# Row sums of the second layer: from four 64x32 tiles of the PE array to all eight, each head's product split by halves of the block's nodes

## The chip, the cores and the metric

The kernel runs on one core of one Trainium2 chip. Its time is device microseconds of one execution. The engines of a core work side by side: TensorE (PE in the profile; PEld is its weight loads), VectorE (DVE), ScalarE (ACT), GpSimd (POOL) and SyncE (SP), each with its own queue of instructions. They wait for one another through semaphores. Matrix products go from on-chip memory (SBUF) into eight banks of accumulators (PSUM, 512 f32 columns by 128 partitions each); DVE and ACT read those, POOL does not.

## The reference

Four graph layers are stacked over 4096 nodes of 256 features, with one 4096 x 4096 0/1 adjacency; after each layer comes `x = layernorm(x + layer(x, adj))`. All is f32. The change lies in the second layer, a multi-head attention with four heads of 64 features:

```
q, k, v = heads(x @ Wq + bq), heads(x @ Wk + bk), heads(x @ Wv + bv)
scores = einsum('hnd,hmd->hnm', q, k) / sqrt(64) + (edge.T - 1) * 10000
attn = softmax(scores, axis=-1)
ctx = einsum('hnm,hmd->hnd', attn, v)
```

The kernel makes the softmax without a maximum per row: it takes the exponential of the scores less one common shift, multiplies by the 0/1 edge and divides at the end by the sum of a row. That sum, one number for each node and head, is what "row sums" means here.

## The kernel before

The four layers follow one another; `additive_heads`, `multi_head_attention`, `additive_one` and `cosine_attention` hold them. Each works block by block: a block is 512 nodes (`QW`, four groups `QB` of 128), and there are eight blocks. In the second layer the other side of the attention is taken 64 nodes at a time, in 64 steps `j` for each block.

A step of the second layer has three parts. `scores` (L578) makes four 64x64 products, one on each quarter of the PE array, into a PSUM tile `p` of two banks: partitions are two halves `c` of 64 neighbours, `r` is the bank, and head `2c + r` (`KC * c + r` in the code) lies at half `c` and bank `r`. ACT takes the exponential in place (L580). `weights` multiplies by the edges on DVE into `prob` (L590) and adds up `prob` for the row sums in `den[b]`: for even `j` with an addition on POOL (L597), for odd `j` with an accumulating DMA that POOL's queue issues (L603). `sums` (L611), three steps later, multiplies `prob` by the values into two accumulator banks. In the steady state PE alternates four matmuls of L578 with four of L611.

While the next block runs, `finish` ends the block before it at fixed steps. At steps 7 and 9 DVE joins the three parts of `den` (L620). At step 12 `row_sums` sums `den` over the 64 partitions of a half: a product with a 64x32 block of ones for each head puts the head's sum for all 512 nodes on 32 equal partitions, and ACT copies the 128 x 512 result to `kept[b][2]` (L630). At step 15 `turned_row_sums` transposes that in four 128x128 pieces (L635), `turned_half` transposes two groups of outputs (L642), `reciprocals` (L648) reads one of every 32 columns into `rden`, and `half` divides (L653) and adds to the features (L656). Step 18 does the other two groups. Later steps make the layernorm; there the small DVE instructions L136 to L139 (`end_root`) refine a square root, and L150 (`begin_root`) begins it.

`halves()` takes one `p` tile, two banks, out of the same pool of three that `scores` uses, and gives out its banks one by one; it is released when the last reader of either bank is done. So a score matmul three allocations later waits for it.

In the loop of the layer the order on PE, DVE and ACT is the order of the code (`manual_schedule`). POOL and SP, and everything in the next layer, are ordered by the scheduler. The last block's end, `tail`, runs inside the third layer: there `bank()` gives one of four banks, and the instructions stand between the third layer's matmuls (L418), its exponential part on ACT (L410) and its weights on DVE (L412).

Of the kernel before, what the change touches and what calls it, by code (L numbers as in the profile page):

```python
# [20 lines left out]
KC = D // P  # L21
QB = 4
QW = QB * P
# [5 lines left out]
def kernel(  # L29
# [27 lines left out]
    nc = tc.nc  # L57
# [14 lines left out]
    ones = const.tile([P, P], FP, name="ones")  # L72
# [398 lines left out]
    def multi_head_attention(w_sb, b_sb, tail, rows_of_den, narrow_edges):  # L471
# [6 lines left out]
        d = D // H  # L478
        G = P // H
# [3 lines left out]
        kept, den, rden, mvs, roots = {}, {}, {}, {}, {}  # L483
        with ExitStack() as lay:
# [7 lines left out]
            with ExitStack() as pro:  # L492
# [6 lines left out]
                def bank():  # L499
                    return ps.tile([P, QW], FP, name="g")  # L500
# [119 lines left out]
                eng.tensor_tensor(den[b][:, 0, :], den[b][:, 0, :], den[b][:, n, :], OP.add)  # L620

            def row_sums(bank, b):
                pd = bank()
                for r in range(KC):
                    for c in range(KC):
                        h = KC * c + r
                        half = slice(c * d, (c + 1) * d)
                        nc.tensor.matmul(pd[h * G:(h + 1) * G, :], ones[half, :G], den[b][half, 0, r * QW:(r + 1) * QW],
                                         start=True, stop=True)
                nc.scalar.copy(kept[b][KC], pd)  # L630

            def turned_row_sums(bank, b):
                pd = bank()
# [11 lines left out]

            def reciprocals(pd, b):
                rden[b] = fin.tile([P, QB, H], FP, name="rden4")
                nc.vector.reciprocal(rden[b].rearrange("p k h -> p (k h)"), pd[:, ::G])  # L648

            def half(po, b, k):  # L650

# [12 lines left out]
            def finish(b, j):  # L664

                rows = [X[:, b * QB + k, :D] for k in range(QB)]
                if j in (7, 9):
                    join_sums(b, j // 2 - 2)
                elif j == 12:
                    row_sums(halves(), b)  # L670
                elif j == 15:
                    bank = halves()
                    pd = turned_row_sums(bank, b)
                    po = turned_half(bank, b, 0)
                    reciprocals(pd, b)
                    half(po, b, 0)
                elif j == 18:
                    half(turned_half(halves(), b, 2), b, 2)
                elif j in (21, 23, 25, 27):
                    k = (j - 21) // 2  # L680
                    if k == 0:
                        mvs[b] = fin.tile([P, QB, 2], FP, name="mv")
                    one_row(mvs[b], k, rows[k])
                elif j == 29:
                    roots[b] = begin_root(mvs[b])
                elif j == 33:
                    end_root(*roots[b])
                elif j in (35, 37, 39, 41):
                    k = (j - 35) // 2
                    scale_row(rows[k], mvs[b], roots[b][1], k)  # L690
# [6 lines left out]
            with tc.manual_schedule(engines=fixed):  # L697
                for i in range(len(units) + LAG):
                    b, j = units[i - LAG] if i >= LAG else (-1, 0)
# [11 lines left out]
        def tail(bank):  # L711
            b = NB - 1
            join_sums(b, 1, nc.gpsimd)
            join_sums(b, 2, nc.gpsimd)
            row_sums(bank, b)
            reciprocals(turned_row_sums(bank, b), b)
            for k in (0, 2):
                half(turned_half(bank, b, k), b, k)
            mv = fin.tile([P, QB, 2], FP, name="mv")
            for k in range(QB):  # L720
                one_row(mv, k, X[:, b * QB + k, :D])
            layernorm_block(b, mv)
# [216 lines left out]
```

## Time and profile before

| what | value |
|---|---|
| median of five runs | 2940.95 us (2939.52 to 2943.2) |
| the profiled execution's own time | 2940.95 us |
| its span | 2939.1 us |
| granted PE clock | 1.00 |
| span of the second layer's loop | about 823 to 1730 us |
| PE busy in the span | 2916.8 us, 99% |
| row-sum matmuls (L628) | 64 records in eight calls |
| ACT copies of the row sums (L630) | 585 ns in the loop, 566 ns in the tail |
| reciprocals (L648) | 248 ns in the loop, 258 ns in the tail |

PE's records overlap where it works on several tiles at once, so the length of a record is not its cost; the distance between the starts of two groups is. The profile prints the shape of a tile as rows*columns (64*32), then the moving operand (64x512). A bracket behind a line gives the idle time of that engine just before it, and who ended it.

### The profile page before, as it was taken

The numbers are of one execution on the slowest core, as the hardware profiler recorded it, in microseconds if no ns is written. First come the engines' busy times: TensorE is split into PE (matmuls) and PEld (weight loads), VectorE is DVE, ScalarE is ACT, GpSimd is POOL, SyncE is SP. The second block draws the span as 40 slices with busy tenths as digits, with TensorE's granted clock in tenths as the row PEclk, the third lists the DMA queues.
The fourth block names the chain that finished last, engine by engine and source line by source line (L and its number), as shares of the span: only waits on it lengthen the run. The fifth ranks groups of instructions, "written<-read, shape, count | busy, mean of one in ns | idle before, by whom it ended". The sixth has DMA issues, their size and how long they took to land.

```text
span 2939.1 us, 50968 instructions
## 1 busy us (share of the span) xinstructions
PE 2916.8 (99%) x20591; PEld 1565.7 (53%) x20591; DVE 1942.0 (66%) x2488; ACT 1668.5 (57%) x2606; POOL 928.3 (32%) x647
## 2 busy tenths in 40 slices
PE   9999999999999999999999999999999999999998
PEld 5333333333643333333333358888887777777776
DVE  7899999997467777877877865555555333333333
ACT  7899999997356666666666654444444222222222
POOL 1000010100068888888889860000000000000000
PEclk9999999999999999999999999999999999999999
DMA  7566666764068888889889877555552343333331
GB/s 197 106 137 137 137 141 141 143 124 83 1 144 190 185 183 189 180 186 190 179 189 187 179 159 140 154 151 151 152 132 53 49 59 58 58 58 58 58 58 29
DMA packets 207166, 374.91 MB, mean 128 GB/s; under 512 B 15073, under 2 KB 90833, under 8 KB 206034
## 3 DMA queue, kind: packets, MB, share of 16 engines
q0 software_dynamic: 102304, 177.77, 38.4%
q1 hardware_dynamic: 104352, 193.62, 21.9%
q8 instruction: 161, 2.64, 0.4%
q14 instruction: 75, 0.61, 0.1%
q10 hardware_dynamic: 274, 0.26, 0.0%
HBM read 317.00 MB, written 21.04 MB: 115 GB/s over the span
## 4 chain that ended last, share of the span: by engine, by line
PE 97%; DVE 2%; ACT 1%; issue 0%; DVEq 0%; ACTq 0%
PE acc L266 23%; PE acc L810 15%; PE p L578 14%; PE acc L611 14%; PE acc L418 8%; PE g L418 7%; PE p L799 4%; PE g L799 3%; PE g L510 2%; PE g L176 1%; PE g L524 1%; PE acc L176 1%; PE g L118 1%; PE acc L761 1%; DVE s L138 1%; DVE prob L590 1%
## 5 line engine op out<-in xcount | busy, mean ns | idle before, releaser
L590 DVE TENSOR_TENSOR prob<-p,mask 128x1024 f32<-128x1024 f32 x512 | 623.1, 1223 | 202.4 <-ACT p L580 198.2
L580 ACT ACTIVATE p<-p,shift 128x1024 f32<-128x1024 f32 x512 | 556.3, 1088 | 333.8 <-PE p L578 333.0
L266 PE MATMUL acc<-prob,V 128*32 128x512 f32 x6144 | 663.8, 592 | 0.0
L597 POOL TENSOR_TENSOR den<-den,prob 128x1024 f32<-128x1024 f32 x248 | 615.2, 2481 | 78.2 <-DVE prob L590 64.2
L255 ACT ACTIVATE prob<-row,dst 128x512 f32<-128x512 f32 x1024 | 635.5, 711 | 0.1
L256 DVE SCALAR_TENSOR_TENSOR prob<-prob,mask 128x2048 f32<-128x2048 f32 x256 | 582.9, 2287 | 25.1 <-ACT prob L255 22.1
L578 PE MATMUL p<-qT,kT 64*64 64x512 f32 x4096 | 532.7, 590 | 6.6 <-DVE prob L590 5.8
L611 PE MATMUL acc<-prob,V 64*64 64x512 f32 x4096 | 531.5, 589 | 0.0
L810 PE MATMUL acc<-X,prob 128*128 128x257 f32 x2048 | 485.7, 380 | 0.0
L810 PEld LDWEIGHTS acc<-X,prob 128*128 128x128 f32 x2048 | 388.5, 190 | 162.1 <-issue 114.1
L803 DVE TENSOR_TENSOR prob<-prob,mask 128x512 f32<-128x512 f32 x256 | 176.4, 691 | 420.1 <-ACT prob L802 418.9
L266 PEld LDWEIGHTS acc<-prob,V 128*32 128x32 f32 x6144 | 197.4, 110 | 451.6 <-issue 433.5
L91 POOL COPY tick<-prob 128x1 f32<-128x1 f32 x35 | 41.7, 1193 | 1017.1 <-DVE prob L256 645.0
L410 ACT ACTIVATE e<-row,dst 128x512 f32<-128x512 f32 x256 | 184.1, 721 | 235.1 <-DVE prob L412 208.0
L611 PEld LDWEIGHTS acc<-prob,V 64*64 64x64 f32 x4096 | 155.9, 133 | 285.3 <-issue 278.1
L578 PEld LDWEIGHTS p<-qT,kT 64*64 64x64 f32 x4096 | 153.7, 133 | 288.3 <-issue 260.6
L412 DVE SCALAR_TENSOR_TENSOR prob<-e,mask 128x512 f32<-128x512 f32 x256 | 176.6, 690 | 174.1 <-PE acc L418 94.0
L748 POOL DMA_DIRECT2D mask<-in_adjT x64 | 47.4, 741 | 641.1 <-DVE prob L803 507.5
L802 ACT ACTIVATE prob<-p 128x512 f32<-128x512 f32 x144 | 85.8, 596 | 256.4 <-PE p L799 242.4
L603 POOL DMA_DIRECT2D den<-prob x240 | 223.0, 929 | 25.8 <-DVE prob L590 20.8
L418 PE MATMUL g<-V,prob 128*128 128x257 f32 x1024 | 226.6, 380 | 0.0
L418 PE MATMUL acc<-V,prob 128*128 128x257 f32 x1024 | 225.1, 380 | 0.0
(151 smaller groups left out, 1965.4 us busy)
## 6 DMA issues: line engine op xcount, KB each, us to landing
mask<-in_adjT SPq DMA_DIRECT2D x256, 512.0 KB
den<-prob POOLq DMA_DIRECT2D x240, 512.0 KB, 5.3
mask<-edges SPq DMA_DIRECT2D x256, 128.0 KB
mask<-in_adjT POOLq DMA_DIRECT2D x64, 512.0 KB, 5.7
edges<-in_adj POOLq DMA_DIRECT2D x32, 512.0 KB, 9.7
den<-prob SPq DMA_DIRECT2D x16, 512.0 KB
row<-far SPq DMA_DIRECT2D x7, 1024.0 KB
X<-in_x SPq DMA_DIRECT2D x7, 512.0 KB
```

The lines of the kernel that those rows point to most:

```text
L255: nc.scalar.activation(z[:, h, :], row[b][:, h, :], AF.Relu, bias=-1.0, scale=dst[:, j, h:h + 1])
L256: nc.vector.scalar_tensor_tensor(z, z, 1.0, mask[m][:, j % MJ, :].unsqueeze(1).to_broadcast([P, H, QW]), OP.add, OP.mult)
L266: nc.tensor.matmul(acc[b][h * G:(h + 1) * G, n, :], part, prob[b, j][:, h, :], start=(j == 0), stop=(j == NT - 1))
L418: nc.tensor.matmul(acc[b][k][:, :D + 1], prob[b, j][:, k * P:(k + 1) * P], V[:, j, :], start=(j == 0), stop=(j == NT - 1))
L578: nc.tensor.matmul(p[c * d:(c + 1) * d, r, :], kT[half, c, j * d:(j + 1) * d], qT[half, c, cols], start=True, stop=True)
L580: nc.scalar.activation(p, p, AF.Exp, bias=shift)
L590: nc.vector.tensor_tensor(z, p, mask[m][:, j % MJ, :].unsqueeze(1).to_broadcast([P, KC, QW]), OP.mult)
L597: nc.gpsimd.tensor_tensor(to, to, flat, OP.add)
L603: nc.gpsimd.dma_start(to, flat, accum_op=OP.add)
L611: nc.tensor.matmul(acc[b][c][r * d:(r + 1) * d, :], V[half, j, r * d:(r + 1) * d], prob[b, j][half, r, :], start=(j == 0), stop=(j == NH - 1))
L799: nc.tensor.matmul(p, T[:, 0, j * P:(j + 1) * P], T[:, 1, cols], start=True, stop=True)
L810: nc.tensor.matmul(acc[b][k], prob[b, j][:, k * P:(k + 1) * P], X[:, j, :], start=(j == 0), stop=(j == NT - 1))
```

## The change

The four row-sum products of a block (64x32 ones by 64x512 sums, all into one bank) become eight products of 256 columns. Product (`r`, `s`, `c`) takes half `c` of the partitions, head `2c + r`, and half `s` of the block's nodes; it goes to column group `g = 2r + s` of the array and into bank `c`. So each of the eight 64x32 tiles of the array has one product, and the two row halves write different banks, of which 256 columns each are used. The result lies in two banks, and two ACT copies of 256 columns put it side by side into `kept[b][2]`. The transposes stay as they are: four of 128x128. Since partition groups now hold (`r`, `s`) and column pieces hold (`c`, pair of node groups), `reciprocals` reads its sixteen columns in another order, in two instructions of eight columns, one for each `s`. In the tail two banks are taken instead of one.

```diff
             def row_sums(bank, b):
-                pd = bank()
+                pds = [bank() for _ in range(KC)]
                 for r in range(KC):
-                    for c in range(KC):
-                        h = KC * c + r
-                        half = slice(c * d, (c + 1) * d)
-                        nc.tensor.matmul(pd[h * G:(h + 1) * G, :], ones[half, :G], den[b][half, 0, r * QW:(r + 1) * QW],
-                                         start=True, stop=True)
-                nc.scalar.copy(kept[b][KC], pd)
+                    for s in range(2):
+                        for c in range(KC):
+                            g = 2 * r + s
+                            half = slice(c * d, (c + 1) * d)
+                            lo = r * QW + s * QW // 2
+                            nc.tensor.matmul(pds[c][g * G:(g + 1) * G, :QW // 2], ones[half, :G],
+                                             den[b][half, 0, lo:lo + QW // 2], start=True, stop=True)
+                for c in range(KC):
+                    nc.scalar.copy(kept[b][KC][:, c * QW // 2:(c + 1) * QW // 2], pds[c][:, :QW // 2])
...
             def reciprocals(pd, b):
                 rden[b] = fin.tile([P, QB, H], FP, name="rden4")
-                nc.vector.reciprocal(rden[b].rearrange("p k h -> p (k h)"), pd[:, ::G])
+                parts = pd.rearrange("p (c k r s g) -> p k c r s g", c=KC, k=2, r=KC, s=2)
+                for s in range(2):
+                    nc.vector.reciprocal(rden[b][:, 2 * s:2 * s + 2, :].rearrange("p k (c r) -> p k c r", c=KC),
+                                         parts[:, :, :, :, s, 0])
```

## The prediction

> **What bounds the kernel now.** I read the page's engine sums and its chain first:
>
> ```profile
> PE 2916.8 (99%) x20591; PEld 1565.7 (53%) x20591; DVE 1942.0 (66%) x2488; ACT 1668.5 (57%) x2606; POOL 928.3 (32%) x647
> ...
> PE 97%; DVE 2%; ACT 1%; issue 0%; DVEq 0%; ACTq 0%
> ```
>
> TensorE (PE) is busy 99% of the span and makes 97% of the chain that ended last: what PE loses or gains in the second layer reaches the end, unless a later wait takes it back. Then the view of the line that changes, L628:
>
> ```profile
> L628 PE MATMUL p<-den,ones x56: 589/601/613, 957.4 to 1642.7; 64*32 64x512 f32 x56
> L628 PE MATMUL g<-den,ones x8: 589/601/613, 1752.8 to 1753.3; 64*32 64x512 f32 x8
> ```
>
> Each call issues four matmuls and leaves eight records, since every f32 matmul appears as two. There are seven calls inside the loop of the layer (56 records) and one in its tail (8). Then the timeline of PE around the first call (columns: start, length, engine, line, record count):
>
> ```profile
> 955.58 1.04 PE L578 MATMUL p<-qT,kT 64*64 64x512 f32 x8
> 956.43 1.04 PE L611 MATMUL acc<-prob,V 64*64 64x512 f32 x8
> 957.40 1.06 PE L628 MATMUL p<-den,ones 64*32 64x512 f32 x8
> 958.39 1.09 PE L578 MATMUL p<-qT,kT 64*64 64x512 f32 x8
> 959.30 1.04 PE L611 MATMUL acc<-prob,V 64*64 64x512 f32 x8
> ```
>
> Read the distances of the starts, not the lengths. L578 to L611 is 0.86 us: four matmuls on four tiles, in two halves of 0.43. The call takes 0.99 us (957.40 to 958.39), L611 before it 0.97 and L578 after it 0.91. Narrower windows put the call's second half at 957.86. So its four 64x32 tiles do run side by side (two half-streams of 0.43), and 0.03 us in front of the second half and 0.10 behind it are the price of a new tile shape. Last the other engines there and the tail:
>
> ```profile
> 958.53 0.58 ACT L630 COPY kept<-p 128x512 f32<-128x512 f32 x1 [0.76 <-PE p L628]
> ...
> 959.55 1.09 ACT L580 ACTIVATE p<-p,shift 128x1024 f32<-128x1024 f32 x1 [0.43 <-PE p L578]
> ...
> 965.38 0.25 DVE L648 RECIPROCAL rden<-p 128x16 f32<-128x16 f32 x1
> 965.62 2.36 POOL L597 TENSOR_TENSOR den<-den,prob 128x1024 f32<-128x1024 f32 x1 [0.33 <-DVE rden L648]
> 965.66 0.70 DVE L653 TENSOR_TENSOR p<-p,rden 128x512 f32<-128x512 f32 x1
> ...
> 966.39 0.69 DVE L656 TENSOR_TENSOR X<-p,X 128x512 f32<-128x512 f32 x1
> ...
> 968.21 1.04 PE L578 MATMUL p<-qT,kT 64*64 64x512 f32 x8
> ```
>
> ```profile
> 1752.78 1.06 PE L628 MATMUL g<-den,ones 64*32 64x512 f32 x8
> ...
> 1753.67 0.72 ACT L410 ACTIVATE e<-row,dst 128x512 f32<-128x512 f32 x1 [1.01 <-DVE prob L412]
> 1753.77 1.57 PE L418 MATMUL acc<-V,prob 128*128 128x257 f32 x6
> ...
> 1754.30 0.57 ACT L630 COPY kept<-g 128x512 f32<-128x512 f32 x1
> ...
> 1755.18 0.60 PE L635 MATMUL g<-ident,kept 128*128 128x128 f32 x4
> 1755.61 1.04 PE L642 MATMUL g<-ident,kept 128*128 128x128 f32 x8
> ```
>
> **The change, part by part.** The sum is made against the profiled execution: 2940.95 us, 1.85 of it around the span of 2939.1. That is also the median of the five runs shown (2939.52 to 2943.2). 0.2%, 5.9 us, is about what a measurement of this kernel can tell from no change. In the built order PE, DVE and ScalarE (ACT) differ in the loop only at the changed instructions; the queues of SyncE and GpSimd (SP, POOL) are the same throughout, and a few PE and ACT instructions change places in the tail.
>
> *Row sums on PE, seven calls.* Four matmuls of 512 columns on four tiles become eight of 256 on eight. A half-stream of 256 columns is priced by L418: ten records of 257 columns from 1756.49 take 2.33 us, less 0.38 for the last one's own length, so 1.95/9 = 0.217 each. If all eight tiles stream together, the call costs 2 x 0.217 + 0.03 + 0.10, plus 0.03 for four more starts 0.007 apart (eight weight loads of a group lie within 0.15 us, each 0.10 long): 0.60. That is 0.39 saved per call. No row shows eight tiles; the widest are the four here and L266's four 128x32 tiles, both at full rate. Bounds: all eight together, -0.39; four at a time, 4 x 0.217 + 0.16 = 1.03, +0.04; two at a time, 8 x 0.217 + 0.16 = 1.90, +0.91. I take the first: L266 already feeds four different moving streams through each row of the array, and here each row again feeds four. 7 x 0.39 = **2.7 us** saved. The number of shape switches stays. Behind each call the loop goes on at PE's pace (0.86 per group of four, ACT idle until PE), and its one later stall, at L138 below, hangs on work that PE feeds, so it moves along with the gain.
>
> *Weight loads and their second pass.* In the trace the second pass's four loads start 0.03 to 0.05 us after the first pass's matmuls, in the same rows, and nothing is lost before the second pass but the 0.03. So I count eight further loads at nothing; if half were exposed (0.10 each, 0.007 apart) it would be 0.13 per call. [...]
>
> *Copies on ACT.* One of 0.585 becomes two of 256 columns. From 272 ns at 128 columns (L765) and 596 at 512 (L802), both out of PSUM, one is 0.38: +0.18 together, -0.09 if they overlap as L410 and L630 do in the tail. Behind them waits L580, which has 0.43 us of idle ahead of it and comes 0.39 earlier with PE, as the copies do. The buffer is next written three allocations on, at 961.88, against copies that end at 959.11. Cost 0; uncovered it would be +0.1 to 0.2 per call.
>
> *Reciprocals on DVE.* 158 ns for one element (L424) and 248 for sixteen give about 0.20 for eight, so two cost 0.40: +0.16 at most. L656 would release the buffer at 967.08 + 0.16 = 967.24 for the L578 at 968.21: about 1 us of slack is left. Cost 0; without that slack +0.16 per call. The new wait of a score matmul for PE as well as ACT is on row sums that ended 4 us before: 0.
>
> *Tail.* PE is ahead of ACT here: the copies start at 1754.30 behind L410, which hangs on DVE's L412, not on the row sums. In the changed order two L418 matmuls, not three, stand between. PE is done with them at 1753.38 + 0.10 + 4 x 0.217 = 1754.35; the first transposes can start at 1754.30 + 0.38 + 0.06 = 1754.74, the others after the second copy, 1755.01 to 1755.28 (two at 0.165 and 0.109). L642 then starts 0.33 before 1755.61, but one L418 matmul (0.43) is still to do: **0.1 lost**. Bounds: 0.4 saved (no wait) to 0.5 lost.
>
> Sum: -2.7 + 0.1 = -2.6, that is **2938.3 us**, 0.09% less.
>
> **The rivals.**
> *Four tiles at a time.* Against it: nothing in the four-tile groups shows a limit; for it: no row shows more than four. 7 x 0.04 plus the tail's 0.1 is +0.4: 2941.3. Two at a time, 8 x 0.91: 2948.2.
> *Slower: the second reciprocal is caught by POOL.* DVE's L138, 4 columns from SBUF to SBUF, takes 2.52 us or more in all seven blocks, beside POOL's L597, and the like L150 0.16:
>
> ```profile
> L138 DVE TENSOR_SCALAR s<-s x7: 2516/2526/2802, 998.5 to 1683.4; 128x4 f32<-128x4 f32 x7
> L150 DVE TENSOR_SCALAR v<-mv x7: 158/160/163, 991.3 to 1676.1; 128x4 f32<-128x4 f32 x7
> ```
>
>  The second reciprocal would start within 0.1 us of POOL's L597 at 965.62. If it must wait out that addition (to 967.98), L656 ends at about 967.98 + 0.2 + 0.73 + 0.69 = 969.6 and PE's L578 starts 1.4 late: 7 x 1.4 - 2.6 = +7, 2948. It decides from about 1 us of delay on. Against it: L653, which reads PSUM like the reciprocal, runs wholly inside POOL's addition at 0.70 us. [...]
> *Faster: L138's collision goes.* It costs PE some 0.85 us per block (L611 at 1000.72 is followed by L578 at 1002.43, 1.71 where 0.86 is usual). Were POOL a few tenths of a microsecond later against DVE, it would vanish: 7 x 0.85 = 6.0 more, 2932.3. Against it: 4 us before, at 994.44, POOL stands idle until DVE's L590, so the two are locked together, 40 us after the row sums.
>
> **How the numbers follow.** Eight together 0.72 (2937.3 to 2939.3, with the tail's bounds and half a microsecond of scatter); exposed loads 0.05, 2939.2; four at a time 0.10, 2941.3; two at a time 0.02; POOL's catch 0.04; L138 freed 0.07. The predicted time is the first case's. The range runs from 2936.5 to 2942: it leaves out 0.13. Slower is 0.06 and faster 0.07 by these cases; the rest, 0.87, within 0.2%.
>
> **What would show it.** Right: the call at about 957.4 starts L578 0.6 us later, its eight first-pass starts within 0.05 us and the second pass 0.24 after the first; L138 still near 2.5 us. Wrong: starts of the eight in groups 0.2 us apart; a reciprocal of over 1 us; a wait of the L578 at 968 us; the seven blocks' distances (114.1 us now) shorter by much more or less than 0.39.

## The result and the profile after

| what | before | after |
|---|---|---|
| median | 2940.9 us (45 runs, 2938.61 to 2943.86) | 2937.74 us (25 runs, 2936.39 to 2939.28) |
| the profiled execution's own time | 2940.95 us | 2938.06 us |
| its span | 2939.1 us | 2936.2 us |

The ratio is 0.9989, 95% interval 0.9984 to 0.9994: the changed kernel is 3.2 us faster, with an interval of 1.8 to 4.7 us. That lies within the 0.2% that the prediction took as the least a measurement of this kernel can tell; the number of executions is what sets it apart from zero.

The page of the changed kernel, its engine sums and its chain:

```profile
PE 2913.1 (99%) x20655; PEld 1564.7 (53%) x20655; DVE 1943.7 (66%) x2496; ACT 1668.7 (57%) x2614; POOL 928.0 (32%) x647
...
PE 97%; DVE 2%; ACT 1%; issue 0%; DVEq 0%; ACTq 0%
```

PE is still the bound. It has 64 more records (eight calls with sixteen instead of eight) and 3.7 us less busy time. The view of the changed line, now L632 (count, then minimum, median and maximum of one in ns):

```profile
L632 PE MATMUL p<-den,ones x112: 376/388/400, 955.9 to 1638.4; 64*32 64x256 f32 x112
L632 PE MATMUL g<-den,ones x16: 376/388/400, 1750.1 to 1750.4; 64*32 64x256 f32 x16
```

The timeline of PE around the first call (start, length, engine, line, records):

```profile
954.98 1.04 PE L611 MATMUL acc<-prob,V 64*64 64x512 f32 x8
955.95 0.66 PE L632 MATMUL p<-den,ones 64*32 64x256 f32 x16
956.54 1.09 PE L578 MATMUL p<-qT,kT 64*64 64x512 f32 x8
957.45 1.04 PE L611 MATMUL acc<-prob,V 64*64 64x512 f32 x8
```

The call takes 0.59 us from start to start (955.95 to 956.54) where it took 0.99. The neighbours are as before: 0.97 and 0.91. The other engines there:

```profile
955.95 0.18 PEld L632 LDWEIGHTS p<-den,ones 64*32 64x32 f32 x16 [0.81 <-DVE prob L590]
...
956.72 0.65 ACT L635 COPY kept<-p 128x256 f32<-128x256 f32 x2 [0.40 <-PE p L632]
...
957.70 1.09 ACT L580 ACTIVATE p<-p,shift 128x1024 f32<-128x1024 f32 x1 [0.33 <-PE p L578]
...
963.52 0.27 DVE L655 RECIPROCAL rden<-p 128x8 f32<-128x8 f32 x2
963.76 2.36 POOL L597 TENSOR_TENSOR den<-den,prob 128x1024 f32<-128x1024 f32 x1 [0.33 <-DMA den<-prob]
963.83 0.70 DVE L661 TENSOR_TENSOR p<-p,rden 128x512 f32<-128x512 f32 x1
...
964.56 0.69 DVE L664 TENSOR_TENSOR X<-p,X 128x512 f32<-128x512 f32 x1
...
966.36 1.04 PE L578 MATMUL p<-qT,kT 64*64 64x512 f32 x8
```

All sixteen weight loads of the call lie within 0.18 us. The two copies end at 957.37, and ACT then still stands idle for 0.33 us until PE. The two reciprocals last 0.27 us together, the last 0.03 of them beside the beginning of POOL's addition. The last reader of the buffer (L664) ends 1.1 us before the score matmul that may wait for it.

Where did the time go? Measured from start to start, the six whole blocks between the first and the last call of the loop took 114.10 us each before, but for one of 114.38, in which L138 took 2.80 us instead of 2.52. Now each takes 113.69 to 113.71. So the step is **0.40 us per block**, and nothing later in a block takes it back. The two profiled spans differ by 2.9 us, which divides so: 1.45 lay already ahead of the first call (957.40 against 955.95), where nothing was changed; 2.7 are the six blocks; 1.5 were lost between the last call and the tail's; 0.2 lie behind that. The 1.5 is 0.40 gained and 1.9 lost. Of the loss, 0.35 is L138, which took 2.87 us in the last block. The other 1.5 comes from L412 in the tail, as these lines of the changed kernel show:

```profile
1740.05 2.34 POOL L620 TENSOR_TENSOR den<-den 128x1024 f32<-128x1024 f32 x1 [8.05 <-DMA den<-prob]
...
1740.42 2.52 DVE L412 SCALAR_TENSOR_TENSOR prob<-e,mask 128x512 f32<-128x512 f32 x1 [1.57 <-PE acc L418]
...
1743.69 1.08 PE L176 MATMUL g<-w_sb,xT 128*128 128x258 f32 x3 [1.56 <-DVE xT L119]
```

and, of the kernel before,

```profile
1742.68 2.35 POOL L620 TENSOR_TENSOR den<-den 128x1024 f32<-128x1024 f32 x1 [7.19 <-DMA den<-prob]
...
1744.61 0.97 DVE L412 SCALAR_TENSOR_TENSOR prob<-e,mask 128x512 f32<-128x512 f32 x1 [1.57 <-PE acc L418]
```

POOL's join in the tail starts when an accumulating DMA has landed, and if the DVE instruction L412 comes up while it runs, L412 waits it out (2.52 us instead of 0.69). In the profiled execution of before it met only the last 0.4 us of the join. This is not the change: in the experiments' profiles the same instruction took 0.69 to 2.43 us, and 2.37 and 1.93 in the two that have the old four tiles. A single pair of profiles can therefore be off by 1.5 us here and by as much in the start.

### The profile page after: what moved, and what is told of

The parts are those of the page before. It is cut to its first block, busy times and chain, and to the rows that moved or that the text cites. A ratio compares the mean times of both kernels' runs of the same rounds, so it can differ in the third digit from the quotient of the medians.

```text
span 2936.2 us, 51125 instructions
## 1 busy us (share of the span) xinstructions
PE 2913.1 (99%) x20655; PEld 1564.7 (53%) x20655; DVE 1943.7 (66%) x2496; ACT 1668.7 (57%) x2614; POOL 928.0 (32%) x647
## 4 chain that ended last, share of the span: by engine, by line
PE 97%; DVE 2%; ACT 1%; issue 0%; DVEq 0%; ACTq 0%
PE acc L266 23%; PE acc L818 15%; PE p L578 14%; PE acc L611 14%; PE acc L418 8%; PE g L418 7%; PE p L807 4%; PE g L807 3%; PE g L510 2%; PE g L176 1%; PE g L524 1%; PE acc L769 1%; PE acc L176 1%; PE g L118 1%; DVE s L138 1%; DVE prob L590 1%
## 5 line engine op out<-in xcount | busy, mean ns | idle before, releaser
L590 DVE TENSOR_TENSOR prob<-p,mask 128x1024 f32<-128x1024 f32 x512 | 622.9, 1223 | 199.6 <-ACT p L580 195.0
L597 POOL TENSOR_TENSOR den<-den,prob 128x1024 f32<-128x1024 f32 x248 | 618.3, 2493 | 75.4 <-DVE prob L590 65.4
L578 PE MATMUL p<-qT,kT 64*64 64x512 f32 x4096 | 532.7, 590 | 6.7 <-DVE prob L590 5.9
L611 PE MATMUL acc<-prob,V 64*64 64x512 f32 x4096 | 531.5, 589 | 0.0
L611 PEld LDWEIGHTS acc<-prob,V 64*64 64x64 f32 x4096 | 155.8, 133 | 285.4 <-issue 278.1
L578 PEld LDWEIGHTS p<-qT,kT 64*64 64x64 f32 x4096 | 153.7, 133 | 285.5 <-issue 255.5
L412 DVE SCALAR_TENSOR_TENSOR prob<-e,mask 128x512 f32<-128x512 f32 x256 | 178.1, 696 | 174.5 <-PE acc L418 94.3
L418 PE MATMUL g<-V,prob 128*128 128x257 f32 x1024 | 226.6, 380 | 0.0
L418 PE MATMUL acc<-V,prob 128*128 128x257 f32 x1024 | 225.1, 380 | 0.0
```

The costliest lines, as they stand in the source:

```text
L418: nc.tensor.matmul(acc[b][k][:, :D + 1], prob[b, j][:, k * P:(k + 1) * P], V[:, j, :], start=(j == 0), stop=(j == NT - 1))
L578: nc.tensor.matmul(p[c * d:(c + 1) * d, r, :], kT[half, c, j * d:(j + 1) * d], qT[half, c, cols], start=True, stop=True)
L590: nc.vector.tensor_tensor(z, p, mask[m][:, j % MJ, :].unsqueeze(1).to_broadcast([P, KC, QW]), OP.mult)
L597: nc.gpsimd.tensor_tensor(to, to, flat, OP.add)
L611: nc.tensor.matmul(acc[b][c][r * d:(r + 1) * d, :], V[half, j, r * d:(r + 1) * d], prob[b, j][half, r, :], start=(j == 0), stop=(j == NH - 1))
```

## The experiments

The line numbers in the lines shown are each kernel's own.

**Eight products on four tiles.**

```diff
-                pds = [bank() for _ in range(KC)]
-                for r in range(KC):
-                    for s in range(2):
+                pd = bank()
+                for s in range(2):
+                    for r in range(KC):
                         for c in range(KC):
-                            g = 2 * r + s
+                            h = KC * c + r
...
-                            nc.tensor.matmul(pds[c][g * G:(g + 1) * G, :QW // 2], ones[half, :G],
+                            nc.tensor.matmul(pd[h * G:(h + 1) * G, lo:lo + QW // 2], ones[half, :G],
```

> The row sums are cut into the same eight products of 256 columns, but each head keeps its old tile, so only four of the array's tiles are used, all in one bank; the result is copied by two ACT instructions of 256 columns; the reciprocals are the old ones. Theory (the gain is that eight tiles stream at once): a call takes 0.13 + 4 x 0.217 = 1.0 us on PE as before the change, and the time stays at that of the kernel before, within 1 us (2940 to 2942). Rival (the gain comes from shorter products or from the split copy, which releases the bank sooner, and not from the number of tiles): a call of about 0.8 us or less and 2937.5 to 2939, as the changed kernel.

Measured: 2941.09 us against 2940.41 for the kernel before on the same chip, ratio 1.0002 (0.9993 to 1.0011). PE around the call:

```profile
955.01 1.04 PE L611 MATMUL acc<-prob,V 64*64 64x512 f32 x8
955.98 1.07 PE L630 MATMUL p<-den,ones 64*32 64x256 f32 x16
956.97 1.09 PE L578 MATMUL p<-qT,kT 64*64 64x512 f32 x8
```

The call takes 0.99 us, exactly as before the change. Halving the products and splitting the copy is worth nothing by itself; the gain is that the other four tiles work too.

**The products five times over, with eight tiles and with four.** In both kernels a loop `for again in range(5):` stands around the products of a call.

> The changed kernel with the eight products of a call issued five times in a row (the result is the same). Theory (eight at once, and PE's time reaches the end one for one): each repeat adds two half-streams of 256 columns, 0.434 us, with no shape switch; 4 x 0.434 x 8 calls = 13.9 us over the changed kernel's 2937.7, so 2951.6, and a call of 0.60 + 1.74 = 2.34 us. Rival (groups of four, and the single call's 0.59 us owes something to its edges): 0.868 per repeat, +27.8 us, 2965.5. Rival (part of PE's time in a call is hidden behind a later wait): less than +10 us.

> The kernel before with the four products of a call issued five times in a row (the result is the same). Theory: each repeat adds two half-streams of 512 columns, 0.858 us; 4 x 0.858 x 8 = 27.5 us over 2940.9, so 2968.4: twice the step of the eight-tile kernel under the same treatment. Rival (time in a call is partly hidden): clearly less than 27 us, at the same share as with eight tiles.

Measured: 2958.09 us with eight tiles (ratio 1.0061, 1.0047 to 1.0075) and 2968.67 us with four (1.0097, 1.0082 to 1.0113). PE around the first call, with eight tiles and then with four:

```profile
955.36 2.39 PE L631 MATMUL p<-den,ones 64*32 64x256 f32 x80
957.68 1.09 PE L578 MATMUL p<-qT,kT 64*64 64x512 f32 x8
```

```profile
955.07 4.50 PE L629 MATMUL p<-den,ones 64*32 64x512 f32 x40
959.50 1.09 PE L578 MATMUL p<-qT,kT 64*64 64x512 f32 x8
```

With four tiles a call takes 4.43 us, 3.44 more, or 0.86 per repeat; blocks are 117.53 us, 3.43 more; the time is 28.3 us over the kernel before's 2940.41 in the same runs, where 27.5 was expected. What PE spends in a call comes out at the end one for one. The two row halves write one bank here, where L578 and L611 write two, and a pair of passes takes the same 0.86 us; so it is not the second bank that makes the changed kernel faster. With eight tiles a call takes 2.32 us, 0.43 per repeat, and the blocks 1.73 more: just half. But the time is 6.5 us above what was expected. The timeline of the tail of that run shows where it goes:

```profile
1760.99 2.39 PE L631 MATMUL g<-den,ones 64*32 64x256 f32 x80
...
1763.47 0.37 ACT L634 COPY kept<-g 128x256 f32<-128x256 f32 x1 [0.86 <-PE g L631]
...
1770.08 0.37 ACT L634 COPY kept<-g 128x256 f32<-128x256 f32 x1 [6.24 <-remote]
...
1770.51 0.69 PE L639 MATMUL g<-ident,kept 128*128 128x128 f32 x2 [5.85 <-ACT kept L634]
```

The second copy starts 6.2 us after the first has ended, and PE waits for it. In the 6.5 us in which PE is busy for 0.66 the mean granted clock is 0.79, in the 3.5 us behind them 0.50, and in the next 4 us 0.93, so that by estimate PE works at half its clock for some 4 us (the view by windows; the third number from the right is the clock):

```profile
1758.00:1764.00 6.00, 6.00 (x98) 4.44 (x97) 2.19 (x4) 2.11 (x6) 0.84 (x1) 1.00 0.11 22
1764.00:1770.50 6.50, 0.66 (x5) 0.32 (x3) 0.00 (x0) 0.37 (x1) 0.00 (x0) 0.79 0.26 22
1770.50:1774.00 3.50, 3.49 (x14) 3.21 (x15) 1.99 (x5) 0.00 (x0) 0.56 (x1) 0.50 0.63 136
1774.00:1778.00 4.00, 4.00 (x23) 3.54 (x22) 4.00 (x13) 1.31 (x2) 0.00 (x0) 0.93 0.29 82
```

At half the clock the eight records of L646 take 1.91 us, where those of L647 took 1.04 in the changed kernel's tail; half of those 4 us, 2.0, is an estimate of what the matmuls there lose besides. In the changed kernel's own tail L412 took 0.7 us more than here and the transposes waited 0.4 us; the wait of 6.0 and those 2.0, less these, come to 6.9 us, against a surplus of 6.5. As for what held the second copy back, the trace shows this much: the last product of the call ends at about 1763.4 and the first copy at 1763.84; the 6.22 us from there to 1770.06 the view of the chain puts down to "another core or an unknown queue", and SyncE's L95 goes on at that moment too (1770.12). So ACT was not the cause; what the copy waited for so long stays open.

**The five repeats in the loop alone.** The tail has its products once: `range(5 if b < NB - 1 else 1)`.

> The changed kernel with the eight products issued five times in the seven calls of the loop alone; the tail has them once. The run with five everywhere was at 2958.1 instead of 2951.6, and its profile shows one wait of 5.8 us in the tail, of the transposes for ACT's copy. Theory (that wait comes from the order of the tail alone): 2937.7 + 7 x 4 x 0.434 = 2949.9. Rival (a part of the surplus comes from the calls in the loop): 2953 or more.

Measured: 2949.21 us, ratio 1.0029 (1.0018 to 1.0040). The long wait is gone, and the 28 extra repeats cost 11.5 us over the changed kernel's median, 0.41 each; the blocks are 1.73 us longer than the changed kernel's, as with five everywhere. The surplus was the tail's alone.

**Four products over all 128 rows.** The weights are a block `pick` of 128x32: ones in the upper half of the rows for columns 0 to 15, in the lower half for columns 16 to 31.

```diff
-                pds = [bank() for _ in range(KC)]
+                pd = bank()
                 for r in range(KC):
                     for s in range(2):
-                        for c in range(KC):
...
+                        g = 2 * r + s
+                        lo = r * QW + s * QW // 2
+                        nc.tensor.matmul(pd[g * G:(g + 1) * G, :QW // 2], pick, den[b][:, 0, lo:lo + QW // 2],
+                                         start=True, stop=True)
-                for c in range(KC):
-                    nc.scalar.copy(kept[b][KC][:, c * QW // 2:(c + 1) * QW // 2], pds[c][:, :QW // 2])
+                nc.scalar.copy(kept[b][KC][:, :QW // 2], pd[:, :QW // 2])
...
-                for k in range(QB):
+                for k in range(2):
                     nc.tensor.transpose(pd[:, k * P:(k + 1) * P], kept[b][KC][:, k * P:(k + 1) * P], ident)
...
-                parts = pd.rearrange("p (c k r s g) -> p k c r s g", c=KC, k=2, r=KC, s=2)
+                parts = pd[:, :QW // 2].rearrange("p (k r s c g) -> p k c r s g", k=2, r=KC, s=2, c=KC)
```

> Another way to the same half-length streams: four products over all 128 rows, 128x32 tiles, with a weight block that sums the upper half of the partitions into 16 columns and the lower half into the other 16. Each of the four column tiles takes one (r, s) of 256 columns; one bank, one ACT copy of 256 columns, two transposes instead of four, the same two reciprocals. Theory (a call's length is the stream length as long as all rows and columns of the array are covered, however many tiles that is): the call takes 0.57 us, the transposes save 2 x 0.109 = 0.22 more, together 0.25 per call against the changed kernel, 7 x 0.25 = 1.8 and up to 0.3 in the tail: about 2935.7. Rival (the number of tiles matters): a call of about 1.0 us, and the time between 2938.5 and 2941.

Measured: 2935.33 us, ratio 0.9983 (0.9974 to 0.9992).

```profile
955.14 1.04 PE L615 MATMUL acc<-prob,V 64*64 64x512 f32 x8
956.11 0.64 PE L632 MATMUL p<-den,pick 128*32 128x256 f32 x8
956.68 1.09 PE L582 MATMUL p<-qT,kT 64*64 64x512 f32 x8
```

The call takes 0.57 us with four products, where it took 0.59 with eight, and blocks are 113.42 us, 0.27 less than with eight tiles: 0.02 of it in the call and most of the rest from the two transposes that go. So it is not the number of tiles that sets the length of a call, but that all rows and columns of the array take part, each column group for half as long.

**The end of the square root one step later.** This prices the stall of the third rival. In `finish`:

```diff
-                elif j == 33:
+                elif j == 34:
                     end_root(*roots[b])
```

> The changed kernel with the end of the square root (L136 to L139 in the profile of the kernel before) moved from step 34 - 1 to step 34 of the next block, so that it stands behind the weights of the other parity on DVE. Theory (L138 is caught by POOL's addition, 2.5 us instead of 0.16, and that makes the one stall of a block on PE): one step later the addition on POOL has about 0.8 us left when the four instructions come up, the rest of them fit between two additions, DVE is 1.0 us late instead of 2.4, and PE does not stall: 7 x 0.85 = 6.0 us less than the changed kernel's 2937.7, so 2931.7. Rival (the stall has another cause, or the instructions are caught again by the next addition): 2936 to 2940, and a wait of PE for DVE of 0.7 us or more in each block as now.

Measured: 2931.64 us, ratio 0.9966 (0.9954 to 0.9979); 6.1 us below the changed kernel's median. The small instructions of the first block on DVE:

```profile
998.24 1.23 DVE L590 TENSOR_TENSOR prob<-p,mask 128x1024 f32<-128x1024 f32 x1 [0.43 <-ACT p L580]
999.38 1.25 DVE L136 TENSOR_TENSOR s<-r 128x4 f32<-128x4 f32 x1
1000.66 0.16 DVE L137 TENSOR_TENSOR s<-s,v 128x4 f32<-128x4 f32 x1
1000.86 0.27 DVE L138 TENSOR_SCALAR s<-s 128x4 f32<-128x4 f32 x1
```

Now L136 is the one that waits for the end of POOL's addition (POOL's L597 runs from 997.96 to 1000.59), 1.1 us, and the others follow between two additions. PE no longer waits in the blocks. Its waits for L590 (us in total, times, the longest), in the changed kernel and then in this one:

```profile
PE p L578 <- DVE prob L590: 5.9, 8, 1.0
```

```profile
PE p L578 <- DVE prob L590: 0.8, 1, 0.8
```

Blocks are 112.79 us, 0.90 less.

**Both together, and the tail's join on DVE.** The first puts the last two edits into one kernel. The second also changes, in `tail`, `join_sums(b, 1, nc.gpsimd)` and `join_sums(b, 2, nc.gpsimd)` to the default engine, DVE.

> The kernel with the row sums over all 128 rows (four products, two transposes) and the end of the square root at step 34. Theory: the two gains are in different places of a block and add: 2935.3 - 6.0 = 2929.3. Rival (one takes back the other through POOL's rhythm): not below 2932.

> As the run before it, and the last block's two joins of the partial sums, in the tail, on DVE (1.22 us each) instead of POOL (2.35 each). Theory (in the tail a weight instruction of the third layer on DVE, L412 in the kernel before, is caught by POOL's join in most executions and costs PE 0.9 to 1.5 us): that collision goes, 1 to 1.5 us less than the run before it. Rival (DVE, which takes its queue in order, now stands waiting for the accumulating DMA that POOL waited for, some 8 us at its longest): no gain, or up to 5 us more.

Measured: 2927.84 us for the two edits, ratio 0.9955 (0.9943 to 0.9967), the best of all kernels here: 13.1 us under the kernel before. With the join on DVE 2940.38 us, ratio 0.9998 (0.9989 to 1.0007). The gains add: blocks are 112.55 us, one of them 112.71, where 0.27 and 0.90 off 113.69 give 112.52. The time is 1.5 us below the 2929.3 expected, which is not explained. The rival for the join was right, only dearer than the 5 us it allowed: 12.5 us over the run without it. The waits of PE and of DVE in that last run:

```profile
PE g L180 <- DVE xT L123: 5.4, 2, 5.0
PE acc L615 <- DVE prob L594: 4.2, 1, 4.2
```

```profile
DVE den L624 <- DMA den<-prob: 9.6, 2, 6.0
```

In this run a join that waits for a DMA held up what stood behind it on DVE: the last weights of the second layer (L594), for which PE then waited 4.2 us, and the next layer's `xT` (L123), for which it waited 5.0. And the 5 us in which PE stood still cost more than 5: from 1732 to 1737.4 us its clock is granted at 0.50, and the sixteen records of L180 behind the wait take 6.59 us, where they take 3.91 in the run with four products over all rows.

## Why the prediction was right

It forecast 2938.3 us (2936.5 to 2942), and 2937.74 was measured. Its signs came out too: the eight first-pass starts lie within 0.05 us, the second pass begins 0.24 after the first, and the blocks are 0.40 shorter. By its own steps:

*Row sums on PE.* Forecast 0.60 us a call and 0.39 saved, on the reading that eight tiles stream together; measured 0.59 and 0.40. The two lower cases (four at a time, 1.03; two at a time, 1.90) are out: a repeat costs 0.43 us with eight tiles and 0.86 with four. The price that was taken from another line's 257-column records, 0.217 per half-stream, holds.

*Weight loads.* Eight more at nothing: right, since 0.59 leaves no place for the 0.13 that exposed loads would have added. All loads end at 956.13 us, 0.06 before the second pass begins, while the first streams in the same rows. The case of exposed loads, 2939.2 us, adds that 0.13 to each of seven calls; no run shows such loads, and the calls were 0.59.

*Copies and reciprocals.* Copies were put at 0.38 us each and cost 0.375; the idle time of ACT behind them shrank from 0.43 to 0.33 and covered them. The reciprocals were put at 0.20 each and cost 0.156 and 0.198, together 0.27. Neither came onto the path: the blocks shortened by the call's whole 0.40.

*Tail.* Forecast 0.1 lost. Between the tail's row sums and the next L176 group there were 8.92 us and now are 8.56, with one matmul of L418 less in between (two records of 0.217). That is 8.99 against 8.92: 0.07 lost. The wait of the transposes for the copy is there as predicted, 0.36 us.

*The sum* was -2.6; the medians give -3.2, and their interval, 1.8 to 4.7 us, holds both. The 0.6 between them can't be told from scatter, since L412's wait alone moves an execution by up to 1.5 us; that the totals agree to 0.6 us is in part luck, and the 0.40 per block is the firmer evidence.

*The rivals.* POOL did not catch the second reciprocal: none in the loop took more than 0.2 us. But the case was hardly put to the test, for in every block of the loop the second reciprocal begins 0.12 us before POOL's addition and is 0.03 us into it when it ends. A lead like that did not save L138, which in one block of each kernel began 0.12 and 0.18 us ahead of the addition and took 2.80 and 2.87. No run had a reciprocal come up in the middle of an addition. The faster case did not come about by the change, since L138 was caught in all seven blocks of the changed kernel:

```profile
L138 DVE TENSOR_SCALAR s<-s x7: 2511/2520/2874, 996.7 to 1678.8; 128x4 f32<-128x4 f32 x7
```

Its price, forecast at 6.0 us, was measured by moving it: 6.1. Its condition, POOL a few tenths of a microsecond later, would not have done. In the first block of the run with eight products on four tiles POOL's addition began 0.5 us after L138, where it usually begins 0.1 before it; L138 escaped, but L139 behind it was caught, and PE waited 1.2 us instead of 0.7:

```profile
997.10 0.17 DVE L138 TENSOR_SCALAR s<-s 128x4 f32<-128x4 f32 x1
997.30 3.02 DVE L139 TENSOR_TENSOR r<-r,s 128x4 f32<-128x4 f32 x1
```

## What to carry to other kernels

On an array that several tiles share, count how many rows and columns take part and for how many columns they stream: a repeat of the products took 0.86 us on four tiles and 0.43 on eight. The number of instructions hardly mattered here, with starts 0.007 us apart. Before the tile map is refined further, see whether the same coverage can be had with fewer instructions and less to do afterwards: four whole-row products took 0.57 us instead of 0.59 and saved two transposes. And a step of half a microsecond that runs eight times is worth 0.1%; the stall of 0.85 us in each block, which the waits of PE showed all along, was worth twice that and one digit of an edit.

## What the runs showed beyond that

- A PE that stood still for 5 to 6 us came back at half its clock for about 4 to 6 us (granted 0.50 in 1770.5 to 1774 of the run with eight products five times over, in 1732 to 1737.4 of the run with the join on DVE). In these two runs a long wait of PE was therefore dearer than its length, in the first of them by an estimated 2.0 us for 6.0.
- Which DVE instruction meets POOL's addition decides what it costs: L138, L139, L136 and L412 read SBUF alone and waited for it (up to 3.0 us for work of 0.16 to 0.69), while L590 and L653, which read PSUM, ran at 1.22 and 0.70 us beside it.
- Two executions of kernels that are alike in the first layer reach the first row sums up to 2.3 us apart (955.07 to 957.40), nearly as much as the whole change is worth. Differences of this size are to be read from block to block inside a trace, and only then from medians.
